# Two graph layers in fp32 on one core: the products split into 64-row halves, the lower half ten units behind

## The chip, the core and the metric

The kernel runs on one core of a Trainium2 chip. The core has a matrix engine (TensorE, "PE" in the profile; its weight loads are listed apart as "PEld"), three engines for elementwise work (VectorE "DVE", ScalarE "ACT", GpSimd "POOL") and a sync engine ("SP") that here only issues transfers. PE reads both operands from on-chip memory (SBUF, 128 partitions) and writes only to PSUM, eight banks of 128 partitions x 512 fp32 values; DVE and ACT carry results from there to SBUF. Transfers (DMA) are issued from the queues of SP, POOL and ACT and share 16 DMA engines.

The metric is the device time of one execution in microseconds (us); smaller is better. Before the change it was 1462.21 us (median of three runs, 1462.16 to 1463.71).

## The reference

Two graph-convolution layers over `x` (8 x 2048 nodes x 64 features) with a 2048 x 2048 matrix `adj`. Each node has its own weights, made from its embedding. Layer 0, with `A = adj`:

```python
w = jnp.einsum('nd,dkio->nkio', embedding, weight)      # per-node weights, D = 16, K = 3
b = jnp.einsum('nd,do->no', embedding, bias)
As = [eye, A, 2.0 * (A @ A) - eye]
x_g = jnp.einsum('knm,bmc->bnkc', jnp.stack(As, 0), x)
out = jnp.einsum('bnki,nkio->bno', x_g, w) + b
x = layernorm(x + out)
```

Layer 1 is the same with its own embeddings and a fourth support, `softmax(relu(E @ E.T), axis=1)`. Both layers end in a residual and a layernorm.

## The kernel before

**Layout.** The eight batches are side by side, so `x` is 2048 rows (nodes) x 512 columns, 16 slabs of 128 rows in SBUF. Instead of `A @ A` the kernel computes `u = A x` and then `A u`. It works in five phases of eight stages, a stage for each block of 256 nodes: A0 (`u = A x` of layer 0), B0 (`A u`), A1 and V1 (the same for layer 1), and between them Z1 (softmax support times x). Stages 0 to 39 run in the order A0, B0, A1, Z1, V1.

**Products of a stage.** A stage needs a 256 x 2048 block of a matrix times 2048 x 512. Most stages do it by Strassen-Winograd in seven products (`strassen`, L504): `times(p)` (L534) runs eight steps over the rows. In the A phases a step is one matmul with 256 columns moving; in the others it is two with 128 (wide Z1 stages: 256). Five "plain" stages do it directly (`straight` L484, `turned` L639). Progress is counted in *units*: a unit is 128 rows x 128 stationary columns x 256 moving columns. A Strassen stage is 56 units long, a plain one 64. fp32 is not one pass on PE: the profile lists two weight loads and two matmuls for each fp32 matmul of the program, so a unit is two passes of 256 moving columns or four of 128. Operands declared F32R (embeddings and weight tables, which are split into a rounded part and a rest stacked over the partitions) take one pass.

**Accumulators.** Two PSUM banks, `acc0` and `acc1` (L89, L480), take turns: one product fills one, while DVE and ACT evacuate the other (`add`, L550). Three double banks (`big`, L96) serve everything else.

**Other work on PE**, placed between the units of the products:

- `weights` (L336): per-node weights, 64-row matmuls in pairs, the first on partitions 0 to 63, the second on 64 to 127, tiles `pw`; a job makes up to three double banks, which ACT and DVE copy to `w`. In six stages an odd pair is put into the idle accumulator, its two halves apart, with a wait between them (`seen`, L356).
- `apply` (L370): 16 groups of 32 stationary columns, tile `po`; then four DVE operations that add to `acc`.
- `turn` (L436): transposes, tile `pt`. `scores`, `numerators` (L689, L702, tile `ps`), `scores_of_rows` (L736, tile `pr`) and `bias` (L323, tile `pb`): F32R matmuls over 128 rows, of which the last 64 hold zeros (L160; `load_s1` L223 fills the first 64).

**The order of the work** is written out by hand: `put(n, i, job)` (L820) places a job at unit `i` of stage `n` (scaled to a length of 64), and the loop at L949 issues the products step by step and every job that has come due. Engines execute in that order (`Pinned`, L33), each its own part of it, so an instruction that waits holds up all behind it on its engine; a DMA queue does the same. Since all operations go through that helper, the profile gives L43 for nearly all; work is told by its tiles.

**Streams.** `adj` (L266, class `Ahead` L235) keeps four tiles of 512 KB (`a`) on SP's queue, quarters of the matrix (`in_adj_q`) or sums that A0 wrote to memory (`sd`). `next` asks for as many loads as buffers are free, when a product starts; `wst` does the same with three tiles of weight tables (`wd`). Results that later stages need pass through memory (`ud`, `zd`, `pd`, `bx`, `cd`). `store_c` (L756) writes a row's maximum and sum to `cd` in elements of 4 bytes, twice in each A1 stage.

The accumulators, as they stand:

```python
def acc_bank(i):
    return ps_acc.tile([P, BC], F32, tag=f"acc{in_use[0] ^ i}", name="pa")
```

Of the kernel before, what the change touches and what calls it, by code (L numbers as in the profile page):

```python
# [9 lines left out]
F32 = mybir.dt.float32  # L10
# [5 lines left out]
P = 128  # L16
N = 2048
B = 8
C = 64
# [10 lines left out]
V1 = C // 4  # L30

# [17 lines left out]
def two_graph_layers(ctx: ExitStack, tc: tile.TileContext, x, x_t, adj_b, adj_q, layers, out):  # L49
# [33 lines left out]
    ps_acc = ctx.enter_context(tc.tile_pool(name="ps_acc", bufs=1, space=PSUM))  # L83
    ps_big = ctx.enter_context(tc.tile_pool(name="ps_big", bufs=3, space=PSUM))

    in_use = [0]
    in_turn = mybir.DependencyInfo(mybir.DependencyClass.Sync, mybir.DependencyReason.DATA)

    def acc_bank(i):  # L89

        return ps_acc.tile([P, BC], F32, tag=f"acc{in_use[0] ^ i}", name="pa")
# [68 lines left out]
    for t in (*bst, s1):  # L160
        nc.gpsimd.memset(t.bitcast(F32), 0.0)
# [4 lines left out]
    for li, (e, b) in enumerate(raw):  # L166
# [5 lines left out]
        for q in range(4):  # L172
            pool.dma_start(out=ed[q * D:(q + 1) * D, :].rearrange("d (c n) -> (d c) n", c=NBLK), in_=eh[q % 2])
            pool.dma_start(out=bst[li][q * D:(q + 1) * D, :].bitcast(F32), in_=bh[q // 2])
# [48 lines left out]
    def load_s1():  # L223
        for q in range(4):
            pool.dma_start(out=s1[q * D:(q + 1) * D, :].bitcast(F32), in_=estk[1][(q // 2) * D:(q // 2 + 1) * D, :])
# [6 lines left out]
    orders = {("V1", 0): (1, 2, 3, 4, 7, 6, 5), ("V1", NBLK - 1): (1, 4, 7, 6, 5, 2, 3)}  # L232
    usual = (1, 4, 7, 2, 6, 5, 3)

    class Ahead:  # L235
# [13 lines left out]
        def next(self, fill=True):  # L249
            if fill or not self.ready:  # L250
                self.fill()
            return self.ready.pop(0)

    def load_adj(t, key):
# [6 lines left out]
        else:  # L261
# [3 lines left out]
    quarters = [("quarter", at) for at in ((0, 0), (1, 1), (1, 0), (0, 1))]  # L265
    adj = Ahead(4, lambda: stream.tile([P, 4 * NB], F32, tag="a", name="a"), load_adj,  # L266
                [key for phase in ("A0", "B0", "A1") for j in range(NBLK)
                 for key in ([("plain", j, i) for i in range(NJ // 4)] if (phase, j) in plain
                             else [(kind, j, i) for kind, i in (quarters if phase == "A0" else
                                                           [factors[p][0] for p in usual])])])  # L270

    def load_last_phase():
        adj.order += [(kind, j, i) for j in range(NBLK) for kind, i in (factors[p][0] for p in orders.get(("V1", j), usual))]
        adj.fill()
# [6 lines left out]
    class Stage:  # L281
# [41 lines left out]
        def bias(self):  # L323
            ps = big("pb")
            for s in range(SB):
                pe.matmul(ps[:, s, 0:C], self.e2[:, s * P:(s + 1) * P], bst[self.li], start=True, stop=True)
# [9 lines left out]
        def weights(self, v0, v1):  # L336
            if v0 == 0:
                self.w = w_room[:, 0:NB * self.units].rearrange("p (n o) -> p n o", n=NB)
                self.ws = {}
            for c in range(v0 // 8, (v1 - 1) // 8 + 1):  # L340
                if c not in self.ws:
                    self.ws[c] = wst.next(fill=False)
            pairs = list(range(v0, v1))
            made = [(v, big("pw").rearrange("p h (v n) -> p h v n", n=NB)) for v in pairs[:-1:2]]
            spare = []
            if len(pairs) % 2:
                spare = [pairs.pop()]
                made.append((spare[0], acc_bank(1).rearrange("p (h v n) -> p h v n", h=2, n=NB)))
            for at in zip(spare + pairs, pairs + spare):
                for h, v in enumerate(at):  # L350
                    r = slice(64 * h, 64 * h + 64)
                    i, ps = (v - v0) % 2, made[(v - v0) // 2][1]
                    ins = pe.matmul(ps[:, h, i, :], self.ws[v // 8][r, v % 8, :], self.e2[r, :], start=True, stop=True)

                    if v in spare and not h:
                        seen = act.activation(small.tile([1, 1], F32, tag="seen", name="seen"), ps[0:1, h, i, 0:1], AF.Copy)  # L356
                    elif v in spare:
                        tc.add_manual_dep(ins.ins, seen.ins.name, in_turn, reason="one bank, two row tiles")
            wst.held = 1 if v1 % 8 else 0
            wst.fill()  # L360
            if spare:
# [658 lines left out]
```

## Time and profile before

| | |
|---|---|
| profiled execution, first to last instruction (its own time) | 1460.9 us |
| timed runs, median (range) | 1462.21 us (1462.16 to 1463.71) |
| PE busy | 1439.2 us, 99% of the span, 13502 matmuls |
| PE weight loads busy | 1186.3 us, 81% |
| DVE / ACT / POOL busy | 971.6 / 485.0 / 208.3 us |
| mean granted PE clock | 0.998 |
| DMA | 285.50 MB, mean 195 GB/s; per-slice busy share 0.3 to 0.9 |

How to read it: "busy" of a group of instructions is the time in which it, and not an earlier instruction of the engine, kept the engine; matmuls overlap in the pipeline, so the mean duration of one is longer than its busy time divided by its count. What one costs is read from the distance between starts in the timeline. A form such as `64*128 64x256` says 64 rows and 128 stationary columns, 256 moving columns.

### The profile page before, as it was taken

How to read it: one execution, taken by the hardware profiler on the slowest of the kernel's cores; microseconds unless marked ns; L12 is line 12 of the kernel's file. 1: busy time of each engine (PE TensorE's matmuls, PEld its weight loads, DVE VectorE, ACT ScalarE, POOL GpSimd, SP SyncE). 2: the span in 40 equal slices, each digit the busy share in tenths (PEclk: the TensorE clock that was granted, in tenths of full speed). 3: DMA queues.
4: the chain of work that ended last, by engine and by line, in shares of the span. 5: the costliest groups of instructions: out<-in, count | busy, mean ns of one | idle time of the engine just before them, and what ended most of it. 6: DMA issues, size and time to landing. Idle time of an engine off the chain costs nothing.

```text
span 1460.9 us, 31574 instructions
## 1 busy us (share of the span) xinstructions
PE 1439.2 (99%) x13502; PEld 1186.3 (81%) x13502; DVE 971.6 (67%) x1647; ACT 485.0 (33%) x639; POOL 208.3 (14%) x343
## 2 busy tenths in 40 slices
PE   9999999999999999999999999999999999999997
PEld 4577777778999998568777777799888988888886
DVE  3866666648676666875566676589794566666666
ACT  0444444432211212154544434612110233333332
POOL 5212221110111111211011111011000000000001
PEclk9999999999999999999999999999999999999999
DMA  9788888886666666578787877323313866666662
GB/s 362 275 265 277 283 288 273 269 314 195 209 192 207 200 199 207 158 177 187 201 191 169 216 203 181 51 74 97 86 44 110 251 181 193 188 194 198 190 200 59
DMA packets 88379, 285.50 MB, mean 195 GB/s; under 512 B 14000, under 2 KB 19632, under 8 KB 86640
## 3 DMA queue, kind: packets, MB, share of 16 engines
q1 hardware_dynamic: 55568, 175.13, 40.4%
q0 software_dynamic: 27200, 94.71, 22.0%
q10 hardware_dynamic: 5472, 13.63, 2.8%
q8 instruction: 107, 1.75, 0.5%
q14 instruction: 32, 0.26, 0.0%
HBM read 217.33 MB, written 62.41 MB: 191 GB/s over the span
## 4 chain that ended last, share of the span: by engine, by line
PE 92%; DVE 3%; DMA 3%; issue 1%; ACT 1%; POOL 0%; ACTq 0%; SPq 0%; DVEq 0%
PE pa L43 67%; PE po L43 13%; PE pw L43 8%; DVE acc L43 1%; PE pt L43 1%; DMA wst<-wd 1%; PE ps L43 1%; PE pr L43 1%; DMA t<-t 1%; DVE w L43 1%; DMA a<-in_adj_q 0%; ACT w L43 0%; DMA sd<-sums 0%; DVE t L43 0%; PE pi L43 0%
## 5 line engine op out<-in xcount | busy, mean ns | idle before, releaser
L43 ACT ACTIVATE w<-pw 128x1024 f32<-128x1024 f32 x309 | 304.7, 1029 | 403.2 <-PE pw L43 400.3
L43 DVE SCALAR_TENSOR_TENSOR acc<-po,mask,acc 128x256 f32<-128x256 f32 (+1 forms) x640 | 246.9, 426 | 67.9 <-PE po L43 57.5
L43 DVE COPY w<-pw 128x1024 f32<-128x1024 f32 x127 | 155.5, 1224 | 196.8 <-PE pw L43 196.5
L43 PE MATMUL pa<-a,u 128*128 128x128 f32 (+1 forms) x2048 | 264.0, 285 | 1.3 <-issue 1.2
L43 PEld LDWEIGHTS pa<-a,u 128*128 128x128 f32 x2048 | 245.0, 192 | 13.8 <-issue 3.8
L43 PE MATMUL pa<-x,a 128*128 128x256 f32 (+1 forms) x816 | 238.7, 436 | 0.0
L43 PE MATMUL po<-w,t 128*32 128x256 f32 (+1 forms) x5120 | 206.5, 337 | 7.3 <-issue 6.3
L43 PE MATMUL pa<-u,a 128*128 128x256 f32 x832 | 203.6, 388 | 0.0
L43 PEld LDWEIGHTS pa<-x,a 128*128 128x128 f32 x816 | 150.7, 190 | 60.3 <-issue 38.4
L43 PEld LDWEIGHTS po<-w,t 128*32 128x32 f32 (+1 forms) x5120 | 129.0, 108 | 78.7 <-issue 14.6
L43 PEld LDWEIGHTS pa<-u,a 128*128 128x128 f32 x832 | 151.3, 190 | 29.4 <-issue 5.4
L43 PE MATMUL pw<-e,wst 64*128 64x256 f32 x1680 | 144.4, 295 | 2.2 <-ACT w L43 1.8
L43 PEld LDWEIGHTS pw<-e,wst 64*128 64x128 f32 x1680 | 111.7, 184 | 33.9 <-issue 17.0
L43 PE MATMUL pa<-a,x 128*128 128x128 f32 x768 | 93.0, 277 | 0.0
L43 PEld LDWEIGHTS pa<-a,x 128*128 128x128 f32 x768 | 88.3, 192 | 2.4
L43 PE MATMUL pa<-w,u 128*128 128x256 f32 x384 | 85.8, 379 | 0.0
L43 PE MATMUL pa<-a,w 128*128 128x128 f32 x672 | 81.3, 277 | 0.0
L43 PEld LDWEIGHTS pa<-w,u 128*128 128x128 f32 x384 | 72.0, 190 | 9.3
L43 PEld LDWEIGHTS pa<-a,w 128*128 128x128 f32 x672 | 77.3, 192 | 2.5 <-issue 1.4
L43 ACT ACTIVATE t<-pt 64x512 f32<-64x512 f32 x64 | 40.8, 638 | 76.8 <-DVE t L43 65.2
L43 DVE TENSOR_TENSOR t<-pa,temps 64x256 f32<-64x256 f32 (+1 forms) x130 | 54.0, 415 | 18.5 <-PE pa L43 16.5
L43 POOL DMA_DIRECT2D e<-ed x80 | 42.2, 532 | 168.0 <-PE pw L43 144.3
(129 smaller groups left out, 1271.9 us busy)
## 6 DMA issues: line engine op xcount, KB each, us to landing
wst<-wd SPq DMA_DIRECT2D x108, 512.0 KB, 6.6
a<-in_adj_q SPq DMA_DIRECT2D x90, 512.0 KB, 5.6
a<-sd SPq DMA_DIRECT2D x88, 512.0 KB, 4.6
sd<-a POOLq DMA_DIRECT2D x24, 512.0 KB, 4.6
bx<-bx POOLq DMA_DIRECT2D x32, 256.0 KB, 5.8
acc<-bx POOLq DMA_DIRECT2D x16, 512.0 KB, 7.2
pd<-acc POOLq DMA_DIRECT2D x16, 512.0 KB, 4.6
acc<-pd POOLq DMA_DIRECT2D x16, 512.0 KB, 8.4
```

The lines of the kernel that those rows point to most:

```text
L43: return self._tc.keep_in_program_order(f(*args, **kwargs))
```

## The change

Every product apart from `apply` becomes two matmuls of 64 rows, one on partitions 0 to 63 and one on 64 to 127, that add into the same PSUM bank. The two are not issued together: `product` issues the upper half, puts the lower one into a queue and issues that lower half which was queued ten units earlier. So at any time the upper half works in one bank and the lower half in another. Where a half takes over a bank from the other, it waits for a `nop` on SP's queue that itself waits for the last matmul of the half before. What follows a product (evacuation, release of the matrix tile, next loads) runs when its lower half is done, ten units later than its upper half. Only stage 0 (`first`) keeps 128-row products.

- PSUM: four accumulators in rotation, two double banks instead of three. Plain stages use all four, one for each quarter of the result, changing every four units.
- `weights` is cut into jobs of one double bank (four 64-row matmuls); 16 jobs for a stage (8 in B0), every two to three units. The odd pair in the accumulator is gone.
- `scores`, `numerators`, `scores_of_rows` and `bias` run in pairs of 64-row matmuls, each over half as many rows as before: `s1` and `bst` now hold the same 64 rows twice, nothing is filled with zeros. `turn` makes 16 half transposes with 64 moving columns instead of 8 with 128.
- `apply` keeps its matmuls, but in the phases A0, A1 and V1 its four calls come as two and two instead of four together.
- A matrix tile is held (`take`) until the lower half is through (`release`); the number of buffers stays 4. `store_u` and the sums of the first block go through POOL's queue instead of SP's. The orders of the seven products and the places of many jobs differ.

By count the program has 11223 matmuls (7855 before), 665 (312) entries on SP that only wait or signal, 369 (330) transfers on POOL and 329 (353) on SP; DVE has 655 (612) two-operand operations and 170 (182) copies; ACT copies 336 (309) double banks of `pw`.

```diff
+HALVES = (slice(0, P // 2), slice(P // 2, P))
+LAG = 10
...
-    ps_acc = ctx.enter_context(tc.tile_pool(name="ps_acc", bufs=1, space=PSUM))
-    ps_big = ctx.enter_context(tc.tile_pool(name="ps_big", bufs=3, space=PSUM))
+    ps_acc = ctx.enter_context(tc.tile_pool(name="ps_acc", bufs=4, space=PSUM))
+    ps_big = ctx.enter_context(tc.tile_pool(name="ps_big", bufs=2, space=PSUM))
...
+    def lower_half(until):
+        while lower and lower[0][0] + LAG <= until:
+            _, acc, of, stop, last, done = lower.popleft()
+            half(acc, 1, *of, False, stop, last and not stop)
+            if done:
+                done()
+
+    def half(acc, h, cols, left, right, start, stop, last):
+        r = HALVES[h]
+        ins = pe.matmul(acc.ap[:, cols], left[r], right[r], start=start, stop=stop)
+        if acc.other:
+            tc.add_manual_dep(ins.ins, acc.other.name, in_turn, reason="one bank, two row tiles")
+            acc.other = None
+        if last:
+            acc.other = sp.nop().ins
+            tc.add_manual_dep(acc.other, ins.ins.name, in_turn, reason="one bank, two row tiles")
+
+    def product(acc, cols, left, right, start, stop, cost, done=None, last=None):
+        last = stop if last is None else last
+        half(acc, 0, cols, left, right, start, False, last)
+        lower.append((clock[0], acc, (cols, left, right), stop, last, done))
+        lower_half(clock[0])
+        clock[0] += cost
...
-        def weights(self, v0, v1):
+        def weights(self, v0):
...
+            ps = big("pw").rearrange("p h (v n) -> p h v n", n=NB)
+            for i in range(2):
+                for h, r in enumerate(HALVES):
+                    pe.matmul(ps[:, h, i, :], self.ws[r, v0 % 8 + i, :], self.e2[r, :], start=True, stop=True)
...
             def times(p):
...
+                        elif self.kk:
+                            for q in range(2):
+                                product(acc, slice(q * P, q * P + P), b[:, q * P:(q + 1) * P], a[:, k, :],
+                                        start and q == 0, stop and q == 1, 0.5, done if q else None)
+                                yield 0.5
+                        else:
+                            product(acc, slice(0, half), a[:, k, :], b, start, stop, 1, done)
+                            yield 1
...
+                self.used(factors[p][2])
+                if not inside or streamed and p in (7, 6, 3, 5):
+                    adj.release()
...
         def scores_of_rows(self, s, h):
             ps = big("pr")
-            for i in range(2):
+            for i, r in enumerate(HALVES):
                 at = (2 * h + i) * 512
-                pe.matmul(ps[:, i, :], self.e2[:, s * P:(s + 1) * P], s1[:, at:at + 512],
-                          start=True, stop=True)
+                pe.matmul(ps[:, i, :], self.e2[r, s * P:(s + 1) * P], s1[r, at:at + 512], start=True, stop=True)
...
-                place_weights(n + 1, (1, 5, 14, 23, 32))
-                turned, bursts, posts = 34.5, (39.5, 39.5, 39.5, 39.5), (51,)
...
+                place_weights(*steps(n, 55, 3, 3), *steps(n + 1, 0, 3, 13))
...
+            turned, bursts, posts = (37.5, (40, 40, 50.5, 50.5), (61,)) if n < 7 else (27, (29, 29, 39, 39), (50,))
...
+            turned, bursts, posts = (16, (40, 40, 50.5, 50.5), (61,)) if st.j < 7 else (15.5, (28, 28, 38, 38), (50,))
...
-            bursts, posts = (4, 4, 4, 4), (15, 19, 23)
+            place_weights(*steps(n, *((12, 3.1), (29, 2.2))[st.j] if st.j < 2 else (21, 2.8) if st.j < 7 else (20, 2.4), 16))
+            bursts, posts = ((7, 7, 18, 18), (29, 32, 35)) if st.j else ((16, 16, 27, 27), (37, 40, 43))
...
+    lower_half(clock[0] + LAG)
+    last.post(0, 8, 16, pool)
     last.post(1, 8, 16)
```

## The prediction

> **What bounds the kernel now.** I read the page first, then the waits of PE, then PE's timeline in a few stages, then the transfers. On the page PE is busy all the time, and the chain that ended last runs through it, mostly through the products `pa`:
>
> ```profile
> PE 1439.2 (99%) x13502; PEld 1186.3 (81%) x13502; DVE 971.6 (67%) x1647; ACT 485.0 (33%) x639; POOL 208.3 (14%) x343
> PE 92%; DVE 3%; DMA 3%; issue 1%; ACT 1%; POOL 0%; ACTq 0%; SPq 0%; DVEq 0%
> ```
>
> PE hardly waits for anybody; its largest waits are
>
> ```profile
> PE po L43 <- issue: 6.3, 8, 1.4
> PE pw L43 <- ACT w L43: 1.8, 3, 0.9
> PE pa L43 <- ACT seen L43: 0.3, 1, 0.3
> ```
>
> So time is won only where PE itself does less. A busy PE is not a PE at its peak: the timeline shows where it is slow. One V1 stage (columns: start, us, then the group; the distance from one start to the next is the cost):
>
> ```profile
> 1215.48 7.11 PE L43 MATMUL po<-w,t 128*32 128x256 f32 x128
> 1222.53 0.50 PE L43 MATMUL pw<-e,wst 64*128 64x256 f32 x4
> 1222.95 2.27 PE L43 MATMUL pa<-a,u 128*128 128x128 f32 x18
> 1225.07 5.30 PE L43 MATMUL pa<-a,x 128*128 128x128 f32 x46
> 1230.30 0.98 PE L43 MATMUL pw<-e,wst 64*128 64x256 f32 x12
> 1231.20 2.27 PE L43 MATMUL pa<-a,x 128*128 128x128 f32 x18
> 1233.32 1.95 PE L43 MATMUL pa<-a,u 128*128 128x128 f32 x16
> 1235.19 0.97 PE L43 MATMUL pw<-e,wst 64*128 64x256 f32 x12
> ```
>
> 64 passes take 7.35 us (1222.95 to 1230.30), 34 take 3.99: so 0.112 us a pass and 0.18 us at the two edges of a run. Four `pw` take 0.42, twelve 0.90: 0.120 us a pair of 64-row matmuls, and 0.18 that does not depend on their number. A group of `pw` among 128-row products costs 0.36 us more than its pairs. An A1 stage shows the wider passes and the smaller jobs:
>
> ```profile
> 788.80 1.24 PE L43 MATMUL pa<-x,a 128*128 128x256 f32 x5
> 789.69 0.81 PE L43 MATMUL pr<-s,e 128*128 128x512 f32 x2
> 790.34 3.18 PE L43 MATMUL pa<-x,a 128*128 128x256 f32 x14
> 793.36 1.04 PE L43 MATMUL pt<-ident,u 128*128 128x128 f32 x8
> 794.23 1.89 PE L43 MATMUL pa<-x,a 128*128 128x256 f32 x8
> ```
>
> 14 passes of 256 columns in 3.02: 0.2156 us each. Five of them end at 789.88, so the two `pr` cost 0.46. The eight `pt` cost 0.87. Four `ps` (967.77 to 968.24 by the same reckoning) cost 0.47, or 0.118 each.
>
> The transfers are the second thing to see. In A0 and A1 the DMA engines are busy 0.74 to 0.89 of most 50 us stretches. After each store to `cd`, elements of 4 bytes, everything crawls for some 8 us (first line: DMA share 0.70 at 48 GB/s; second: a normal stretch):
>
> ```profile
> 795.00:803.00 8.00, 8.00 (x56) 6.25 (x56) 2.45 (x2) 6.75 (x10) 0.00 (x0) 1.00 0.70 48
> 805.00:809.00 4.00, 4.00 (x27) 3.02 (x25) 1.98 (x3) 1.98 (x3) 0.73 (x1) 1.00 1.03 398
> ```
>
> **The change part by part.** The sum is made against the profiled execution, span 1460.9 us, 1.3 below the median of the timed runs (1462.2); I apply the difference to the median.
>
> *`pw` without edges.* By the cuts in the code there are 162 groups: 6 in stage 0, 5 in each of six stages, 6 in each of 17, 3 in each of eight. Where all neighbours are 64-row too, the edges have no cause: 162 x 0.36 = 58 us less. The pairs themselves stay.
>
> *Half the rows.* 32 `pr` pairs: 0.46 becomes one matmul's time, taken as twice 0.120 for twice the columns, so 0.24: 7 us less. 128 `ps` at 0.118 become 64 pairs at 0.120: 7 less. `pb` is too small to count.
>
> *Transposes.* 24 times 0.87. Half the columns move, with as many loads; `pt` loads are short (140 ns against 190 for the others). Between 0.48 (half) and 0.87; I take 0.6, as the load is the shorter part: 6 less (0 to 9).
>
> *The products' passes.* 3584 of 128 columns, 2384 of 256, 128 of 512 that become 256. Each becomes two half passes that should run side by side. No row shows fp32 halves with 128 stationary columns. The nearest: a `pw` pair (256 columns in one pass, 128 columns loaded) takes 0.120, a 128-row `ps` of the same form 0.118; the half-row `po` of B0 (64x32, fp32 with two passes) repeats its eight tiles every 0.218 us for two passes, or 0.109 a pass of 128 columns. The ends are thus -3 and +8 ns a pass, -18 and +49 us for 6100 passes. I take +1.5 ns, the difference between `pw` and `ps`, which have the same load: +9.
>
> The Trainium skill, TensorE: Matmul & The Clock Gate, section LDWEIGHTS, speaks against this: a load costs by its columns, not its rows, 107 ns for 128. If the loads of two halves went one after the other, each of the 3584 narrow passes would take one load more: an estimate of +383 us by that page. In the `pw` row two loads and two matmuls fit into 0.120. TensorEngine Tiling, Instruction Overhead, gives some 60 cycles for each matmul; for 6100 additional ones I estimate 150 us from it, if they could not overlap. The B0 row has 126 half matmuls in 2.02 us, 16 ns each.
>
> *More bursts of `po`.* In 24 stages four applications together become two and two. One burst of 128 takes 7.05 where 32 rounds of 0.2156 are 6.90, and the edges of the next run add 0.18: 0.33 each, 24 x 0.33 = 8 us more.
>
> *The end.* The last ten units of lower halves run alone: 10 x 0.448 = 4.5 us more before the last additions. At the start nothing is lost twice; stage 0 stays as it is.
>
> *Hand-over of banks.* 353 more entries on SP. A half that takes over has two units, 0.86 us, between the end of the last upper half and its own start, for PE to SP to PE. The nearest row is `seen` (PE to ACT to PE), which has 0.82 us (first lone half at 119.26, second at 120.08) and cost PE 0.3 us in all 24 cases. SP does nothing but issue (0.33 us a load), so I take nothing. If that cover is gone, each tenth of a microsecond costs 35 us.
>
> *Longer holding of tiles.* The load for product k+4 was asked for when k+1 started, 24 units before use; now after the lower half of k, 14 units before. Followed load by load in A1, the shortest time from issue to first use was 12.84 us, and in each stage one load landed only 2.0 to 2.7 us before use, after 11 to 12 us under way, in the stretch slowed by `cd`. That load had 13.8 us and will have 8.0. With two loads under way instead of three it should land about 1.3 us earlier (512 KB at 398 GB/s): late by some 2 us, in 7 stages: 14. In A0 the last tile of a stage is freed when ten units of the next are done and needed 14 units later through a DVE subtraction (1.2 us); landings there are 3.5 to 8 us: 1 us in 6 stages, 6. V1 lands in 3.2 to 5.5 us, B0 mostly in 4 to 8: nothing. Bounds: 0, and the longest landing (14.65 less 7.5) in each A1 stage, 50, with 3 us in each A0 stage, 18.
>
> *Two double banks instead of three.* A `pw` job comes every 2.1 to 3 units, 1.1 to 1.5 us with its own 0.24; ACT copies it in 1.03 us, DVE in 1.22. With two banks that is covered as long as DVE is not late with a `po` or a copy; late are then `pw` and, behind it on PE, the products. 5 us, between 0 and 20.
>
> *DVE* does about the same work; it would be busy 68% instead of 67%.
>
> Sum: 1462 - 58 - 14 - 6 + 9 + 8 + 4.5 + 0 + 20 + 5 = 1430 us.
>
> **The rivals.**
>
> 1. *No new wait.* The order was laid out so that loads and banks are in time; then the last two terms vanish: 1405 us, and 1378 with the passes at 0.109 (-18 in place of +9). For it: V1 and Z1 have slack. Against it: the `cd` stretches, which no order removes.
> 2. *The tile window takes it all* (the other side). Without new waits the gain is 57 us; from 4.4 us in each of the 13 Strassen stages of A0 and A1 on, the change loses. At the upper bound, 50 + 18 + the 5 for banks, it is 1478. For it: landings of 10 to 14.65 us in A1 against windows of 7.5 to 8; DMA share 0.89 in A0. Against it: those long landings are partly the queue of three loads, and the windows with a `po` burst inside are 3.5 us longer.
> 3. *The hand-over is late.* SP's entries stand in one line with loads that wait for buffers; if a `nop` comes 0.3 us late on average, 353 x 0.3 = 106 us: 1536. For it: two units are little. Against it: `seen`.
> 4. *The halves do not run side by side* in fp32 with full columns, so that the change does not do what it says: each narrow pass 0.224, +400 us, 1830. Against it: both half-row rows. Hardly 1 in 100.
>
> **How the numbers follow.** Forecast (1415 to 1457) 0.50; rival 1 (below 1415) 0.20; rival 2 (1466 to 1495) 0.17; rivals 3 and 4 (above) 0.08; the rest, 0.05, lies where gain and waits cancel within 0.2%, about what a measurement of this kernel can tell from no change. Faster: 0.50 + 0.20 = 0.70; same 0.05; slower 0.17 + 0.08 = 0.25. The range leaves out rival 3 and the outer ends: 1387 (rival 1 with passes 1.5 ns shorter than now instead of longer, 3 ns x 6100) to 1492 (rival 2, with passes 2 to 3 ns longer). The forecast's own range is 1415 to 1457.
>
> **What would show it.** `pw` groups of four with about 0.24 us between the neighbouring `pa`, no edge. Two half passes of `pa`, upper and lower, starting every 0.113 (128 columns) and 0.217 us (256). PE idle before `pa` released by DMA `a`, some 20 us in A1 and A0, after each `cd` store; more than 60 means rival 2. PE waiting for SP: rival 3. `pr` under 0.25 us a pair. `po` bursts of 64 in 3.6 us. DVE busy near 970 us. The prediction is wrong first of all if a pass of halves differs from 0.112 by more than a few ns: 1 ns is 6 us.

## The result

The changed kernel takes 1613.53 us (median of four runs, 1610.4 to 1614.66) against 1462.18 us (1460.99 to 1463.71) of the kernel before beside it: a ratio of 1.103, 95% interval 1.1017 to 1.1048. The forecast was 1430 us, the range 1387 to 1492. It is slower by 151 us, beyond the forecast and all rivals but the last (1830 us), which the profile excludes below.

The first part and the chain of the page of the kernel after; all operations now have L46:

```profile
PE 1448.9 (90%) x20046; PEld 1243.1 (77%) x20046; DVE 973.8 (60%) x1674; ACT 508.0 (32%) x624; POOL 228.1 (14%) x379
PE 39%; DVE 10%; ACT 5%; issue 2%; DMA 2%; POOL 0%; ACTq 0%; DVEq 0%; POOLq 0%
```

PE is busy for as long as before (1439.2), but in a span of 1610.8 us instead of 1460.9: it now stands still for 162 us, before for 22 (in both, some 9 to 12 us of that lie behind its last matmul). The share of PE in the chain fell from 92% to 39%. Whom it waits for, the largest rows of the waits of PE (us in total, times, longest):

```profile
PE pw L46 <- ACT w L46: 24.4, 17, 2.5
PE pw L46 <- DVE w L46: 22.3, 14, 4.6
PE po L46 <- DMA t<-t: 15.6, 7, 2.8
PE pt L46 <- ACT w L46: 13.0, 6, 2.2
PE pb L46 <- ACT w L46: 8.8, 7, 1.3
PE pa L46 <- DMA a<-sd: 4.3, 1, 4.3
PE pa L46 <- DMA a<-in_adj_q: 4.0, 3, 2.7
```

No row is large and none names SP. The largest part, 69 us in the four rows of `pw`, `pt` and `pb`, is one thing: a job that needs a double bank which ACT or DVE has not emptied. The rest is spread over some 25 rows of transfers and operands that come late at the new places, the copies `t<-t` of B0 before all. One of them in the V1 stages, the timeline of DVE, ACT and PE (start, us, group, and in brackets the idle time before and what ended it):

```profile
1402.23 1.21 DVE L46 TENSOR_REDUCE mean<-acc 128x16 f32<-128x1024 f32 x1
1403.68 1.22 DVE L46 TENSOR_TENSOR acc<-acc,mean 128x1024 f32<-128x1024 f32 x1
...
1399.79 1.02 ACT L46 ACTIVATE w<-pw 128x1024 f32<-128x1024 f32 x1 [0.40 <-PE pw L46]
1404.99 1.06 ACT L46 ACTIVATE sq<-acc 128x1024 f32<-128x1024 f32 x1 [4.18 <-DVE acc L46]
1405.96 0.35 ACT L46 COPY temps<-pa 128x256 f32<-128x256 f32 x1
1406.21 1.03 ACT L46 ACTIVATE w<-pw 128x1024 f32<-128x1024 f32 x1
...
1404.60 0.27 PE L46 MATMUL pa<-a,x 64*128 64x128 f32 x1
1407.29 0.50 PE L46 MATMUL pw<-e,wst 64*128 64x256 f32 x4 [2.42 <-ACT w L46]
```

ACT's square of the layer norm waits 4.18 us for DVE's mean and subtraction. Behind it on ACT stand the copies of two `pw` jobs that PE finished meanwhile. With three double banks a third job would have had room; with two, PE stops for 2.42 us, and with it all products that are queued behind the `pw`. The same happens once in nearly every stage of A0, A1 and V1, each phase with its own culprit: in A0 DVE's copy of `pw` behind two subtractions of matrix tiles (2.5 us), in A1 ACT's copies behind two exponentials (2.3 us).

The second half of the loss was in nobody's list. The same place in five windows of the trace (PE, PEld, DVE, ACT, POOL busy, then the granted PE clock, the DMA share and GB/s):

```profile
1397.50:1400.91 3.41, 3.41 (x64) 3.41 (x62) 1.45 (x3) 2.42 (x3) 0.00 (x0) 1.00 0.50 155
1400.91:1404.32 3.41, 3.41 (x66) 3.41 (x64) 3.17 (x4) 0.00 (x0) 0.00 (x0) 1.00 0.27 85
1404.32:1407.74 3.42, 1.00 (x16) 0.81 (x15) 1.86 (x3) 2.64 (x5) 0.00 (x0) 1.00 0.60 230
1407.74:1411.15 3.41, 3.41 (x38) 3.41 (x35) 2.24 (x3) 1.73 (x2) 1.19 (x1) 0.50 0.00 0
1411.15:1414.56 3.41, 3.41 (x64) 3.41 (x64) 1.16 (x3) 2.05 (x2) 0.00 (x0) 1.00 0.87 229
```

In the third window PE was busy for 1.00 us of 3.42. In the fourth it is busy throughout, but at a granted clock of 0.50 it starts 38 matmuls where the windows around it have 64. The trace's clock records show this in 38 windows of 3.41 us, all on one grid; the profile before has none (every profile ends at half clock, but behind PE's last matmul). A window in which PE is busy throughout costs half of its length, 1.71 us.

So the time can be taken apart: span, less the time in which PE was not busy (span minus PE busy, both on the page), less 1.71 us for each half-clock window. What remains is PE's own work at full clock: 1460.9 - 21.7 = 1439 before, 1610.8 - 161.9 - 64.9 = 1384 after. The price of 1.71 us is somewhat too high, since PE also stood still in some of the 38 windows: counting only its busy time there, they cost 59 us, and 1390 remain. So the change did take 49 to 55 us off PE's work, not far from the 56.5 that the sum had without its terms for waits. The loss is 140 us of standing still and 59 to 65 us of half clock.

### The profile page after: what moved, and what is told of

The parts are those of the page before. It is cut to its first block, busy times and chain, and to the rows that moved or that the text cites. A ratio compares the mean times of both kernels' runs of the same rounds, so it can differ in the third digit from the quotient of the medians.

```text
span 1610.8 us, 45103 instructions
## 1 busy us (share of the span) xinstructions
PE 1448.9 (90%) x20046; PEld 1243.1 (77%) x20046; DVE 973.8 (60%) x1674; ACT 508.0 (32%) x624; POOL 228.1 (14%) x379
## 3 DMA queue, kind: packets, MB, share of 16 engines
q0 software_dynamic: 30320, 104.71, 21.7%
## 4 chain that ended last, share of the span: by engine, by line
PE 39%; DVE 10%; ACT 5%; issue 2%; DMA 2%; POOL 0%; ACTq 0%; DVEq 0%; POOLq 0%
PE pa L46 28%; PE po L46 6%; DVE w L46 3%; PE pw L46 3%; DVE acc L46 2%; ACT w L46 2%; ACT sq L46 1%; DMA a<-sd 1%; DVE row L46 1%; ACT row L46 1%; DVE t L46 1%; ACT t L46 1%; DVE mean L46 1%; DVE u L46 1%; DMA c<-cd 0%
## 5 line engine op out<-in xcount | busy, mean ns | idle before, releaser
L46 ACT ACTIVATE w<-pw 128x1024 f32<-128x1024 f32 x336 | 340.8, 1023 | 456.4 <-PE pw L46 449.7
L46 PE MATMUL pa<-a,u 64*128 64x128 f32 (+1 forms) x4096 | 422.4, 285 | 6.4 <-DMA u<-ud 4.9
L46 PE MATMUL pa<-x,a 64*128 64x256 f32 (+1 forms) x1824 | 399.1, 399 | 9.8 <-DMA a<-in_adj_q 4.0
L46 PEld LDWEIGHTS pa<-a,u 64*128 64x128 f32 x4096 | 391.2, 192 | 14.8 <-issue 10.9
L46 DVE SCALAR_TENSOR_TENSOR acc<-po,mask,acc 128x256 f32<-128x256 f32 (+1 forms) x640 | 249.5, 426 | 182.3 <-PE po L46 171.8
L46 PE MATMUL pa<-u,a 64*128 64x256 f32 x1664 | 352.6, 398 | 4.3 <-DMA a<-sd 4.3
L46 PEld LDWEIGHTS pa<-x,a 64*128 64x128 f32 (+1 forms) x1824 | 270.5, 193 | 44.1 <-issue 18.0
L46 PE MATMUL pw<-e,wst 64*128 64x256 f32 x1728 | 244.3, 358 | 52.3 <-ACT w L46 24.4
L46 PEld LDWEIGHTS pa<-u,a 64*128 64x128 f32 x1664 | 244.0, 196 | 28.9 <-issue 8.2
L46 PE MATMUL po<-w,t 128*32 128x256 f32 (+1 forms) x5120 | 221.5, 354 | 27.6 <-DMA t<-t 15.6
L46 DVE COPY w<-pw 128x1024 f32<-128x1024 f32 x112 | 136.9, 1223 | 143.8 <-PE pw L46 143.2
L46 PEld LDWEIGHTS pw<-e,wst 64*128 64x128 f32 x1728 | 158.4, 197 | 79.8 <-ACT w L46 32.1
L46 PEld LDWEIGHTS po<-w,t 128*32 128x32 f32 (+1 forms) x5120 | 136.5, 114 | 100.4 <-issue 20.0
L46 PE MATMUL pa<-a,x 64*128 64x128 f32 x1536 | 176.2, 278 | 0.0
L46 PEld LDWEIGHTS pa<-a,x 64*128 64x128 f32 x1536 | 164.5, 193 | 2.9 <-issue 2.9
L46 PE MATMUL pa<-a,w 64*128 64x128 f32 x1344 | 146.8, 277 | 5.8 <-issue 5.8
L46 PEld LDWEIGHTS pa<-a,w 64*128 64x128 f32 x1344 | 139.0, 191 | 8.6 <-issue 8.6
L46 PE MATMUL pa<-w,u 64*128 64x256 f32 x768 | 124.5, 385 | 5.5 <-DVE t L46 5.5
L46 PEld LDWEIGHTS pa<-w,u 64*128 64x128 f32 x768 | 105.4, 191 | 13.4 <-issue 6.2
L46 PE MATMUL pa<-w,x 64*128 64x256 f32 x576 | 105.3, 376 | 0.0
L46 ACT COPY temps<-pa 128x256 f32<-128x256 f32 x58 | 21.3, 366 | 231.9 <-PE pa L46 219.0
L46 PEld LDWEIGHTS pa<-w,x 64*128 64x128 f32 x576 | 87.6, 187 | 5.0 <-DVE temp L46 0.2
```

The lines of the kernel that those rows point to most:

```text
L46: return self._tc.keep_in_program_order(f(*args, **kwargs))
```

## The experiments

Theory: PE stops because two double banks do not cover a copy that stands behind other work on ACT or DVE, and a pause that takes half of one window of 3.41 us lets the clock fall in the next. Rivals: the half clock comes from the 64-row products; the waits, once moved, only turn up elsewhere; tiles of the matrix given back later are the cause.

All runs, worked out as above. The time is the median of the timed runs; the columns behind it are of the one profiled execution, which in a0 was the slower of two (1591.75 us). The last column is what remains for PE's own work:

| run | time, us | span | PE not busy | half-clock windows | remains |
|---|---|---|---|---|---|
| before | 1462.2 | 1460.9 | 21.7 | 0 | 1439 |
| after | 1613.5 | 1610.8 | 161.9 | 38 | 1384 |
| p1_one_pause | 1632.1 | 1626.4 | 137.1 | 32 | 1435 |
| p2_two_pauses | 1615.0 | 1611.3 | 141.8 | 12 | 1449 |
| b3_small_jobs | 1563.8 | 1561.9 | 14.9 | 0 | 1547 |
| b2_small_jobs_two_banks | 1616.5 | 1615.4 | 50.4 | 4 | 1558 |
| f1_full_rows | 1708.2 | 1702.2 | 109.3 | 22 | 1555 |
| a0_copies_on_act | 1585.8 | 1589.9 | 149.0 | 33 | 1385 |
| v1_square_later | 1578.4 | 1580.5 | 146.0 | 30 | 1383 |
| v2_waits_moved | 1538.5 | 1535.0 | 118.1 | 16 | 1390 |
| v3_c_stores_late | 1501.7 | 1502.4 | 89.8 | 13 | 1390 |
| v4_b0_loads_apart | 1486.3 | 1484.2 | 82.0 | 5 | 1394 |
| v5_b0_thinned | 1465.6 | 1463.5 | 66.4 | 4 | 1390 |
| v6_last_waits | 1460.0 | 1454.9 | 61.4 | 3 | 1388 |

For all kernels with the halves of the change the last column is nearly a constant, 1383 to 1394, and 1387 to 1394 if only the busy time of half-clock windows is priced: idle time and half clock account for the differences between them.

### The clock by itself: pauses in the kernel before

```diff
+    scratch = const.tile([P, 256], F32, tag="scratch", name="scratch")
+    def pause(n):                     # the next matmul waits for n fills on POOL
+        last = pe.last
+        for i in range(n):
+            made = pool.memset(scratch, 0.0)
+            if i == 0:
+                tc.add_manual_dep(made.ins, last.ins.name, in_turn, reason="pause")
+        pe.after = made
...
+    for n in range(1, len(stages)):
+        for place, count in ((28, 7),):              # p2: ((16, 3), (40, 3))
+            put(n, place + 0.01, pause, count)
```

> The kernel before, with one pause of PE in each of the stages 1 to 39: at place 28 the next matmul waits for seven small fills on POOL that start after the last matmul, about 2.5 us. Nothing else is changed, and the products have 128 rows. Theory (a pause of over about 1.7 us inside one window of 3.41 us lets the clock be granted at half in the next window): 39 x 2.5 = 98 us of idle time, and a half-clock window after some 70 per cent of the pauses (those that lie mostly in one window), 27 x 1.7 = 46 us: 1605 us, mean granted clock about 0.97. Rival (the half clock comes from the 64-row products, and a pause costs its own length): 1560 us, clock 1.0.

> The kernel before, with two pauses of about 1.3 us in each of the stages 1 to 39 (three fills each, at the places 16 and 40) instead of one of 2.5. Theory: as much idle time in sum, 78 x 1.3 = 101 us, but no window loses half of its work, so the clock stays at 1.0: 1563 us. If the sum of the idle time counted, and not its place in a window, the clock would fall as with one pause: about 1605 us.

Measured: 1632.06 us for one pause and 1615.04 for two. The pauses came out at 2.6 to 3.0 us in 31 places of p1 and at 1.17 to 1.23 in 65 of p2; where POOL stood behind a transfer they were longer (in p1 seven of 3.5 to 4.2 and one of 9.6 us, in p2 twelve of 1.6 to 3.1 and one of 13.3), which is why both runs lie above their expectation. The clock tells them apart. Two pauses of p1, each in its windows (columns as above):

```profile
97.23:100.64 3.41, 1.07 (x5) 0.96 (x6) 1.80 (x3) 0.00 (x0) 1.95 (x7) 1.00 1.02 227
100.64:104.05 3.41, 3.41 (x19) 2.45 (x18) 1.15 (x1) 1.74 (x4) 0.00 (x0) 0.50 0.44 162
...
179.16:182.57 3.41, 1.91 (x8) 1.34 (x8) 3.26 (x6) 1.99 (x3) 1.21 (x4) 1.00 1.01 281
182.57:185.98 3.41, 1.96 (x14) 1.53 (x16) 1.02 (x1) 0.00 (x0) 1.22 (x4) 1.00 0.96 273
185.98:189.40 3.42, 3.42 (x31) 3.03 (x27) 2.85 (x3) 2.80 (x4) 0.23 (x1) 1.00 0.55 194
```

The first pause, 3.02 us, lies mostly in one window (PE busy 1.07 of 3.41) and the next window runs at 0.50. The second, 2.95 us, is divided by the grid (busy 1.91 and 1.96) and nothing happens. Of the 31 pauses of 2.6 to 3.0 us in p1 16 were followed by a fall, and so were all eight longer ones. None of the 65 short pauses in p2 was; all of its eight falls came after the longer ones. Over the three traces (after, p1, p2) a fall followed 63 windows, with PE busy for 0.01 to 0.55 of them; no window below 0.42 stayed without a fall, and none above 0.55 had one. In the other nine traces with falls it is the same: 96 falls, up to 0.54, and none missing below 0.41. The products of p1 and p2 have 128 rows: it takes no halves to lower the clock.

The Trainium skill, TensorE: Matmul & The Clock Gate, section What's actually happening, describes this gate: a free-running window of 3413 ns and half clock after an idle one. The grid of 3.41 us agrees. Its section HAM oscillation gives as the rule of thumb no idle gaps above some 3.4 us; here gaps of 2.4 us, on an otherwise full PE, were enough when they fell into one window, which then was not idle: in the one of V1 above PE was busy for 1.00 us of 3.42.

### The third double bank by itself

As a control the kernel before with `pw` in jobs of one bank, like those of the change, and then the same with two double banks:

```diff
-        cuts = (0, 2, 8, 14, 20, 26, 32) if ... else (0, 6, 12, 18, 24, 28, 32)
+        cuts = range(0, st.units // 2 + 1, 2)
-                on_dve = k == (0 if self.phase == "V1" else len(made) // 2) and ...
+                on_dve = v0 % 8 == 4 and ...
...
-    ps_big = ctx.enter_context(tc.tile_pool(name="ps_big", bufs=3, space=PSUM))
+    ps_big = ctx.enter_context(tc.tile_pool(name="ps_big", bufs=2, space=PSUM))   # b2 only
```

> The kernel before, with its three double banks, but pw in jobs of four matmuls that fill one double bank, spread over the same part of a stage as before, every fourth copied by DVE. A control for the next run. 378 more groups of pw with edges of 0.36 us among 128-row products: 136 us more, about 1600 us, few waits, clock 1.0.

> The control with two double banks instead of three and nothing else changed. Theory (with two banks a copy that stands behind one other operation on DVE or ACT stops PE): 40 to 110 us more than the control, waits of pw, pt, ps, pb for DVE and ACT, and some half-clock windows. By the 5 us that the prediction gave to two banks (bound 20): less than 20 us more.

The control took 1563.78 us. I had miscounted its groups: 24 stages of 16 jobs and eight of 8 are 448, so 286 more than before, and 286 x 0.36 = 103 us gives 1565, which is what it took. With two banks it took 1616.52 us: 52.7 more for one bank less, 35.5 of it standing still, 5 to 7 four half-clock windows, and most of the rest `po`, which takes 211 us by the distances between starts against 201. Waits of PE in the run with two banks; the control's largest is 2.2:

```profile
PE po L43 <- DVE acc L43: 12.2, 23, 0.5
PE pr L43 <- DVE sq L43: 11.1, 8, 6.5
PE po L43 <- ACT t L43: 6.2, 7, 0.9
```

The bank alone costs ten times what the prediction gave it, in an order of work that was made for three. Which job waits differs from the kernel after, as the places differ.

### The halves by themselves

```diff
     def product(acc, cols, left, right, start, stop, cost, done=None, last=None):
-        half(acc, 0, cols, left, right, start, False, last)
-        lower.append((clock[0], acc, (cols, left, right), stop, last, done))
-        lower_half(clock[0])
-        clock[0] += cost
+        pe.matmul(acc.ap[:, cols], left, right, start=start, stop=stop)
+        if done:
+            done()
```

> The kernel after with the one thing undone that its name is from: each product again one matmul of 128 rows, at the place of its upper half, with no lag and no hand-over of banks; four accumulators, two double banks and all jobs stay where they are. Some 576 groups of four pw then stand among 128-row products, each with edges of 0.36 us: 207 us more. Theory (the waits come from two double banks and the places of the jobs, not from the halves): the waits of pw, pt and pb and half-clock windows are still there, partly covered by the longer pw groups: 1750 to 1820 us. Rival (the half clock comes from 64-row products): no half-clock window; 1746 or less.

Here two quarters of the matrix change places in A0, since the additions now come before the next load: the kernel no longer computes the layers of the reference, but does the same amount of work. It took 1708.23 us, below the expected range, by the same miscount of groups (448 x 0.36 = 161 us, not 207); the remaining work is 1555 against 1384, 171 more. With 128-row products there are still 22 half-clock windows, and `pw` and `pt` still wait for ACT; the largest waits of PE are

```profile
PE po L46 <- DVE t L46: 34.4, 7, 5.5
PE pw L46 <- ACT w L46: 19.7, 13, 3.0
PE pw L46 <- DMA wst<-wd: 11.3, 1, 11.3
PE pt L46 <- ACT w L46: 11.0, 12, 1.3
```

So the waits for banks belong to the banks and places, not to the halves. The first and third row are f1's own and were not followed up. The halves themselves earn what the small jobs would otherwise cost.

### Taking the waits away, one phase at a time

```diff
-            copy(v0 % 8 != 4, dst, ps.rearrange("p h v n -> p n v h"))
+            copy(self.phase == "A0" or v0 % 8 != 4, dst, ps.rearrange("p h v n -> p n v h"))
```

> The kernel after, with the copies of pw in the A0 stages all on ACT (there every fourth was on DVE, where it stands behind subtractions of matrix tiles, 2.5 us). Theory (two double banks do not cover a copy that stands behind other work; each such wait costs its length and mostly a window at half clock): the waits of pw for DVE in A0, 19 us in the profile after, go, and with them 8 half-clock windows, 14 us: about 1581 us. Rival (the waits cost their length alone): 1595. Rival (the waits only move to the next late engine, ACT): 1613.

The square apart from the first part of the norm:

```diff
-                act.activation(self.sq[:, s0:s1, :].rearrange("p s o -> p (s o)"), flat, AF.Square)
+                if not (self.phase == "V1" and g == GROUPS):
+                    self.square(s0, s1)
...
+            if phase == "V1":
+                posts = (posts[0], posts[0] + 8, posts[0] + 12)
+                put(n + 1, posts[0] + 4.5, st.square, 0, GROUPS)
```

> The kernel after, with ACT's square of the layer norm in the V1 stages issued 4.5 places later, behind two more copies of pw, and the two later parts of the norm moved back by 5 and 6 places. In the profile after, ACT waits 4.2 us for DVE before this square, with copies of pw behind it, and PE waits 2.43 us in each stage. Theory: six waits (14 us) and five half-clock windows (8.5 us) go: about 1591 us. Rival (the waits cost their length alone): 1600. Rival (the waits only move): 1613.

1585.82 us (ratio to before 1.0743 to 1.0942) and 1578.41 (1.0723 to 1.0861). In A0 the waits of `pw` for DVE are gone and in V1 those for ACT: a V1 stage fell from 40.8 us to 36.5, by 2.4 us of waiting and 1.7 of half clock. The waits hardly moved on within these phases (in A0 one of 3.7 us came up before `pb`); the totals fell by 28 and 35 us. The first median is nearer to the theory (1581) than to the rival without the clock (1595), but its two runs, 1579.90 and 1591.75, lie 12 us apart, and the profile of the slower one shows five windows fewer, not eight. The second is below both, since eight half-clock windows went instead of five.

### All phases

`v2` moves the jobs in every phase; its main lines beside those of the two kernels above:

```diff
+            if self.phase == "A1":
+                on_act = i not in ((7, 10, 13, 14) if self.j == 0 else (7, 13, 14))
+            else:
+                on_act = self.phase == "A0" or self.n == 32 or i % 4 != 2
...
-                bursts, posts = ((16, 16, 30, 30) if st.j else (22, 22, 34, 34)), (42, 45, 48)
-                put(n + 2, 2, st.load_x, range(SB))
+                bursts, posts = ((20, 20, 33, 33) if st.j else (22, 22, 34, 34)), (42, 45, 48)
+                put(n + 2, 14, st.load_x, range(SB))
...
-            put(26 + c, 40 + part, split_weights, part, 1, 1, c)
+            put(at[2], at[3] + part, split_weights, part, 1, 1, c)
```

> The kernel after with its products, halves and banks unchanged, and the jobs that PE waited for moved in every phase: copies of pw in A0 on ACT, in A1 on DVE where ACT has two exponentials ahead, the V1 square later, the po bursts of B0 four places later and its loads of x behind the copies t<-t, A0's last stage in an order that frees the room of u earlier, the row scores of A1's first stage later, the splits of the last weights out of the busy Z1 stages. Theory (idle time of PE and the half-clock windows it causes are the whole loss; the halves themselves gain some 50 us): of 137 us more idle time some 100 go, of 38 half-clock windows some 30, 51 us: about 1460 us. Rival (idle time alone): about 1510. Rival (the waits only move on): 1580 to 1610.

1538.54 us, between the theory and the rival that the waits move on. 44 us of idle time went, not 100. The waits of PE in v2 show why:

```profile
PE pa L46 <- DMA a<-sd: 27.4, 14, 6.1
PE po L46 <- issue: 11.7, 11, 4.6
PE pa L46 <- issue: 9.9, 5, 3.0
PE pw L46 <- ACT w L46: 8.1, 18, 1.0
PE pa L46 <- DMA a<-in_adj_q: 6.0, 4, 3.8
```

The waits for banks are down to single microseconds. In their place PE waits for tiles of the matrix, 33 us. In the kernel after these waits were 8 us; there, presumably, PE came late to the same tiles anyway. The two rows with `issue`, 21.6 us, name nobody: what PE waits for in them the runs do not show.

The next kernel moves most of the stores to `cd` out of A1, where they are followed by a stretch in which all transfers crawl, and with them the load of x of B0's results, two sums and one bias; the main lines:

```diff
-            put(n + 1, 24, st.store_c)
+            put(*((18, 24), (20, 24), (24, 14), (24, 50), (25, 20), (25, 55), (26, 30), (27, 30))[st.j], st.store_c)
...
-                put(n + 2, 14, st.load_x, range(SB))
+                put(n + 2, 2 if st.j == 6 else 49, st.load_x, range(SB))
```

> v2 with the transfers moved that PE now waits for: six of the eight stores to cd leave A1 for the Z1 stages, x of B0's results is loaded after the norm of the stage and not at its start, two sums and one bias come at other places, the po bursts of A0 two places later. Theory (the waits for a<-sd in A1, 27 us in 14 waits in v2, come from the crawl after each store to cd and from loads that come in one burst): about 25 of them and 10 of the other 60 us go, with most of the 16 half-clock windows, 20 us: 1480 to 1490 us. Rival (a tile given back ten units later is simply too late, whatever else is under way): the waits for a<-sd stay above 20 us, 1520 or more.

1501.72 us. The waits of PE for `a<-sd` within 640 to 960 us, the time of A1, first in v2 and then in v3:

```profile
PE pa L46 <- DMA a<-sd: 22.1, 9, 6.1
```

```profile
PE pa L46 <- DMA a<-sd: 1.0, 2, 0.6
```

A stage of A1 fell from about 45 us to 40.5 (distances of the `po` bursts). The rival is out: given back ten units later, the tiles are late only where other transfers stand beside them. The stores to `cd` are part of that. Two pairs of them stayed in A1 (725.7 and 733.5, 806.8 and 814.7 us), and the only two waits left there, 0.61 and 0.38 us, come 12 us behind these two pairs. In v2 the waits at that distance were 2.3 to 3.2 us, so the other transfers that were moved count as well; the run does not separate them. But in B0 the same wait rose from 2.1 to 12.8 us, and with it the run missed its 1480 to 1490: loads of x, of the old sums and copies `t<-t` still start there together. POOL issues the old sums, place 30, at 490.0 us, right behind the copy `t<-t` of 489.5, with which the stage begins, and x, place 49, at 481.6, right behind the store of 480.4 and 5 us before the copies of the next stage: the place in the order did not keep them out of the burst.

```diff
-                pool.dma_start(out=X[SB * self.j + s], in_=nodes[s * P:(s + 1) * P, :])
+                by.dma_start(out=X[SB * self.j + s], in_=nodes[s * P:(s + 1) * P, :])   # by = act in B0
...
-    put(4, 48, load_s1)
+    for i in range(4):
+        put(10 + i, 34, load_s1, range(2 * i, 2 * i + 2))
```

> v3 with the loads of B0 taken out of the burst at the start of each stage: x, the old sums and the stacked embeddings are issued by ACT at places 28, 50 and 34, and stage 0's bias stands six places earlier. Theory (the waits for a<-sd in B0, 15 us in v3, and the wait of 4 us in A0's stage 5 come from transfers that share the DMA engines): some 20 us of idle time and half of the 13 half-clock windows, 11 us, go: about 1470 us. Rival (ACT's issues hold up copies of pw): 1495 or more, with waits of pw for ACT.

```diff
+    for i in range(8):
+        put(8 + i, 48, load_s1, [i])
...
+                for s in range(SB):
+                    put(n + 2, 2 if st.j == 6 else (28, 44)[s], st.load_x, [s])
...
+                put(n + 1, 21, wst.fill, 1)
+                put(n + 1, 45, wst.fill, 1)
```

> v4 with the rest of B0 thinned: its loads of x one by one at places 28 and 44, the embeddings one in each of eight stages at place 48, the weight blocks loaded at places 21 and 45 instead of at the stage's edge; in A1 one of the two copies after the turn on DVE, and the first stage's row statistics four places earlier. Theory (what is left are waits for single transfers in B0 and for ACT in A1): of 69 us idle some 20 go, with three of five half-clock windows, 5 us: about 1461 us, that of the kernel before. Rival (what is left in B0 is not these transfers): 1480 or more.

1486.25 and 1465.56 us. v4 lies between theory and rival: of 20 us of idle time 8 went, and three waits of about 3 us came some 4 us behind pairs of loads that ACT now issued at one place (the profile gives them as `issue`, without a releaser). v5, which spaces them, came near what the theory said (1461), and these waits are gone: from the last product of A0 to the first of A1 it takes 288 us instead of 304 (284 before the change).

```diff
-                    copy(s, dst, src)
+                    copy(0 if self.phase == "A1" and feature is None else s, dst, src)
...
+            order = (0, 8, 4, 12) if self.half else (0, 4, 8, 12)
+            for m0, (group, release) in zip(order, moving):
...
-            turned, bursts, posts = (16, (40, 40, 50.5, 50.5), (61,)) if st.j < 7 else ...
+            turned, bursts, posts = (14.6, (40, 40, 50.5, 50.5), (61,)) if st.j < 7 else ...
```

> v5 with what still waits moved once more: B0's first stage takes its groups of rows in the order 0, 2, 1, 3 so that the slabs of u loaded last are used later (wait of 2.7 us and a half-clock window), the turn of A1 comes 1.4 places earlier with all its copies on DVE and one job of pw 1.4 places later (six waits of 1.0 us), the first copy of pw in A1's first stage is on DVE (2.0 us), two stores of weights in stage 1 come later (2.5 us). Theory: some 10 us of idle time and two of four half-clock windows, 3 us, go: about 1452 us, 0.7 per cent under the kernel before. Rival (other waits take their place): 1463 or more.

1460.02 us (twelve runs, 1456.55 to 1465.42) against 1463.06 of the kernel before (seventeen runs): a ratio of 0.998, interval 0.9967 to 0.9992. It is the first version under both kernels, but by 0.2 per cent, too little to call it faster; the expected 1452 was not reached. The first part and the chain of its page, and the second largest row of PE's waits:

```profile
PE 1393.5 (96%) x20046; PEld 1212.3 (83%) x20046; DVE 943.3 (65%) x1664; ACT 531.0 (36%) x634; POOL 212.8 (15%) x351
PE 66%; DVE 11%; DMA 6%; ACT 3%; issue 2%; POOL 0%; ACTq 0%; DVEq 0%; POOLq 0%
PE pa L46 <- SPq L46: 5.5, 2, 4.2
```

61 us of standing still are left, against 22 before the change, in many waits of about 1 us and one of 4.2. That one is the hand-over of banks through SP: SP issues a load of `wst` at 55.95 us, after waiting for its buffer, the `nop` stands behind it, and PE goes on at 56.46. Waits of 2.9 and 2.4 us at the same place are in v4 and v5. So of the 51 us that PE's work became shorter, 45 are still paid back.

## Why the prediction was wrong

**What bounds the kernel.** Right for the kernel before, though the list of PE's largest waits leaves out three rows of 0.7 to 1.2 us. The step from there, that time is won only where PE itself does less, hid that PE's 22 us of standing still rested on the third double bank.

***pw* without edges: 58 expected, 21 measured, together with the passes.** The price was right. From steady run to steady run a group of 8 costs 0.86 us and one of 12 1.10 in the kernel before, and one of 4 0.63 in b3: 0.38 to 0.39 more than the pairs, whatever their number. In the kernels with halves the edges are gone, as forecast: four `pw` away from other jobs and waits cost 0.235 us, in A0 and A1 as in V1. Yet, adding up the distances between starts less idle time, `pa` and `pw` together take 1164.5 us before and 1143.9 in v6. A part of the difference are PE's stops: at each the profile counts the last matmul to its end as busy, 0.2 to 0.3 us more than its share of the pace, and v6 has 76 stops behind `pa` and `pw` (18 us) where the kernel before had 11 (2 us). The half-clock windows of v6 are 4 to 5 us more; for the remaining 17 us no cause is shown.

**The passes.** +9 expected, 0 measured. Steady runs in the trace of after: 111.7 ns for 128 columns and 215.8 for 256, those of before to the tenth. Two halves side by side, in v6 (timeline of PE):

```profile
1400.28 0.27 PE L46 MATMUL pa<-a,x 64*128 64x128 f32 x1
1400.29 0.27 PE L46 MATMUL pa<-a,u 64*128 64x128 f32 x1
1400.39 0.27 PE L46 MATMUL pa<-a,x 64*128 64x128 f32 x1
1400.40 0.27 PE L46 MATMUL pa<-a,u 64*128 64x128 f32 x1
```

Every 0.11 us an upper and a lower half start, 0.01 us apart, with operands of two different products. Rival 4 is out, and so are the two estimates that the prediction made from the Trainium skill (+383 and +150 us): at this pace nothing of a second load or of an overhead for each matmul is seen.

**Small jobs.** `pr`, `ps` and `pt`: 20 expected, 27 measured (21.0 to 12.6, 21.1 to 11.3, 21.0 to 12.4 us, by distances between starts, before against v6).

**More bursts and the end.** +8 and +4.5 expected; two bursts of 64 take 3.79 each against 7.14 for one of 128, and all `po` 205.6 us against 203.3: +2. From the start of the last matmul to the end 12.6 us instead of 9.8: +3. All terms of PE's own work came to -56.5; measured were -49 to -55.

**Hand-over of banks.** 0 expected; no row of PE's waits in the kernel after names SP. Rival 3 is out as the loss, but what it described does occur: the 5.5 us of v6 are a `nop` behind a load that waits for its buffer.

**Longer holding of tiles.** 20 expected. In the kernel after 8.3 us, but v2, with the other waits gone, shows 33.4, of which 22.1 in A1 (14 expected) and 5.3 in A0 (6 expected). v3 agrees with the cause that was named for A1, the stretch slowed by the stores to `cd`, as a part of it. The mechanism was right and its size fair; it was covered by larger waits. Rival 2, which needed it to be the whole loss, is out.

**Two double banks instead of three: the step that failed.** "That is covered as long as DVE is not late with a `po` or a copy ... 5 us, between 0 and 20". The bank alone costs 53 us in b2 against b3, in an order made for three. In the kernel after the waits of `pw`, `pt` and `pb` for banks come to 69 us, and all of PE's standing still to 140 more than before. I compared one copy (1.03 us on ACT) with the distance between two jobs (1.1 to 1.5 us) and took that for cover. The question was how long the longest thing is that can stand before a copy in the queue of ACT or DVE, a wait included: 4.2 us for the square and 2.5 for two subtractions of tiles, against one job's distance. The operations stood in the profile before: in its V1 stage at 1228.19 us the square waits 2.55 us for DVE, and a subtraction of tiles on DVE takes 1.21. That it is the bank and the places together, v2 shows: with the same two banks and the jobs moved the waits for banks are single microseconds. The other half of the 140 us, the late transfers and operands, had no term but the 20 us for tiles.

**The clock: no step at all.** The granted clock was 1.0 throughout before, so I multiplied no pause by anything. 38 windows at half clock cost 59 to 65 us. The pauses of p1 show that this comes with 128-row products too, and that of two pauses of equal length one can cost its own length and the other 1.7 us more.

Sum: -49 (own work), +140 (standing still), +59 (clock) = +150 us, the difference of the two profiled spans.

## What to carry to other kernels

This is drawn from one kernel. Where a resource with n buffers loses one, add up for each engine that empties them the longest chain that can stand before a copy, waits for third engines included, and compare it with n - 1 distances of the producer; the mean load of that engine said nothing here (DVE 60%, ACT 32% in the kernel after). Price a stall of a full PE at its length, plus half a clock window when it leaves PE busy for less than about half of one window. When the largest wait is removed, look at once for the one that it covered: here bank waits covered tile waits, and those covered bursts of transfers.

## What the runs showed of the hardware

- The granted clock falls to 0.50 for a window of 3.41 us after a window in which PE was busy for less than about half (63 falls in after, p1 and p2, busy share up to 0.55; none missing below 0.42). It stayed there for another window when PE was busy for less than 0.8 to 0.9 of the first. Pauses of 1.17 to 1.23 us, 65 times, never did it; of pauses of 2.6 to 3.0 us in p1 16 in 31 did, as the grid cut them, and all eight of 3.5 us and more.
- fp32 halves of 64 rows with 128 stationary columns run two at a time at the pace of one 128-row pass: 111.7 ns for 128 moving columns and 215.8 for 256, in the kernel after as in v6.
- A group of 64-row matmuls among 128-row ones costs 0.38 us more than its pairs, whether it has 4, 8 or 12 (b3, before); among 64-row ones nothing more (0.235 us for four, after and v6).
- A queue whose engine has little to wait for runs ahead of PE: the place of a load in the order then sets its rank in the queue, not its time. In v3 POOL issues the old sums, place 30, at the start of the stage (490.0 us). ACT, whose copies wait for PE, issues the loads of v5 at places 44, 48 and 50 at 454.1, 456.5 and 456.9 us, 1 to 2 us behind the `pw` jobs beside them (place 43 at 452.2, place 50 at 455.4), but that of place 28 at 437.4, 11 us ahead of the `pw` job of place 36 (448.5).
